# Storing the neighbour mask and the removed mask, and combining them and their transposes on TensorE

## The chip, the cores and the metric

The kernel runs on one core of a Trainium2 chip. The time is the device time of one execution in microseconds (us); lower is better. The engines named below are TensorE (PE; PEld is its weight load), VectorE (DVE), ScalarE (ACT), GpSimd (POOL) and SyncE (SP), whose queue issues all of the kernel's DMAs.

## What is computed

Four graph layers follow each other over 16 batch entries ("elements") of 1024 nodes with 64 features. The change concerns layer 0. It thins the adjacency matrix and then takes, for each node and feature, a weighted mean of three quantiles over the neighbours that are left:

```python
eye = jnp.eye(N, dtype=bool)
adj_ = jnp.where(eye[None], 1.0, adj)
nb = (adj_ > 0) & (~eye)[None]
m = nb.sum(-1)
rank = jnp.cumsum(nb, axis=-1) - 1
skip = jnp.where(m > T_THRESH, (m + K_DIL - 1) // K_DIL, 1)
do_dil = (skip > 1) & mask
removed = nb & do_dil[..., None] & ((rank + 1) % skip[..., None] == 0)
rem = removed | jnp.swapaxes(removed, 1, 2)
adj_d = jnp.where(rem, 0.0, adj_)
...
agg = _weighted_nanquantile_agg(x, adj_d > 0)
```

So an edge is dropped if either of its ends drops it, and the diagonal always stays. Each row drops at most two neighbours. Layers 1 to 3 (a degree-normalised sum, an attention with 8 heads, a linear graph layer) use the adjacency matrix as it came.

## The kernel before

Layer 0 of one element is 96 **compare steps**: 8 groups of features, times two halves of 512 nodes (`t`), times 6 quantile positions. A step makes three wide VectorE products (`le` L798, `wa` L800, `wb` L802), 17 matmuls into `prep` and `val`, two copies on ScalarE, and then `bit`, `pz` and `vs` with some delay. Between them stands the making of the tables (`px`, L710 to L741).

Everything else is interleaved with these steps by Python generators. In each step the loop in `picks` advances:

- the next tables (`coming`), twice;
- the **background** of the next element (`behind`), once. It consists of two generators: `ranking`, which sorts the features of a pair of elements (`ranks`; some 56 turns fall to each element), and `thinning`, which is `dilate`. While both have work, `going[n % 3 // 2]` gives two turns of three to `ranking` and one to `thinning`; when one ends, the other has every turn;
- in the last 12 steps of an element, the **stages** of the next one (`stages`), by the table `STEPS`. They call `neighbours` and `positions`;
- layers 1 to 3 of the element before (`layers`), by a due amount of 0.42 a step.

In the 12 steps before the end of an element the rest of the background is run out, if any is left. For the first element the background and its stages run ahead of the first step. A scheduler then orders the instructions of each engine from what was emitted; each engine and SP's queue take their instructions in that order.

**`dilate(b)`** works on 8 blocks of 128 rows. VectorE makes the mask `nb` of the neighbours without the diagonal (L453, L454), its running count `cum` (a scan, L456), and small columns: `m`, `do`, `mi` and `sk` (L459 to L470). From the row's count the columns `sk[:, 1:2]` and `sk[:, 2:3]` are made such that the entries to drop are those where |cum + sk1| equals sk2. ScalarE takes the absolute value (L471, recorded under the helper's line L379), VectorE compares (L474) and multiplies with `nb` (L475), which gives the mask `rem` of what this row drops. It is stored to `rem_d`. VectorE then subtracts `rem` from `nb` (L477) and adds the diagonal block (L478), and what is left is stored to `left_d`. The generator hands over after the absolute value, after L478 and after the last store: three times per block.

**`neighbours(left_d, rem_d, t)`** makes the mask that layer 0 uses, transposed: for each of 8 column blocks `j` a tile `valid[:, j, :]` of 128 x 512. It loads four 128 x 128 blocks of `left_d` (one DMA of 256-byte rows, L490) and a 128 x 512 piece of `rem_d` (L494) into one buffer `lr`. On TensorE, `minus_i` (the negative identity) takes `rem` into the PSUM tile `pn` as it lies (L499), and four matmuls with the blocks of `left` as weights and the identity as moving operand add the transposed rest (L504). ScalarE writes `valid` as the positive part of `pn`. There are 16 such groups per element, 256 in all.

`b2_` hands out buffers of a ring of six, which `nb`, `cum`, `rem`, `lr`, the sort's tiles and tiles of the layers share; `pb` hands out one of two PSUM tiles.

Of the kernel before, what the change touches and what calls it, by code (L numbers as in the profile page):

```python
# [8 lines left out]
F32 = mybir.dt.float32  # L9
BF = mybir.dt.bfloat16  # L10
# [6 lines left out]
OP = mybir.AluOpType  # L17
# [4 lines left out]
P = 128  # L22
# [16 lines left out]
def tile_preln_adj_stack(  # L39
# [30 lines left out]
    nc = tc.nc  # L70
    B, N, D = x.shape
    C = N // P
# [6 lines left out]
    const = ctx.enter_context(tc.tile_pool(name="const", bufs=1))  # L79
    dram = ctx.enter_context(tc.tile_pool(name="dram", bufs=2, space=DRAM))  # L80
# [13 lines left out]
    def b2_(name, shape=(P, 512), dt=F32):  # L94
        return sb.tile(list(shape), dt, tag="b2", bufs=6, name=name)
# [16 lines left out]
    def pb(name, shape=(P, 512), dt=F32):  # L112
        if alone and name != "pcols":
            return pa(name, shape, dt)
        return ps.tile(list(shape), dt, tag="pb", bufs=2, name=name)

    def small(name, shape, dt=F32, bufs=3):
        return sb.tile(list(shape), dt, tag="s_" + name, bufs=bufs, name=name)
# [26 lines left out]
    def scaled(name, shape, dt, src, scale):  # L145
        t = const.tile(list(shape), dt, name=name)
        nc.scalar.activation(t, src, AF.Copy, scale=scale)
        return t

    ident = scaled("ident", (P, P), HP, identf, 1.0)  # L150
    minus_i = scaled("minus_i", (P, P), BF, identf, -1.0)
    less = const.tile([P, 2, P], HP, name="less")
    nc.scalar.activation(less[:, 0, :], identf, AF.Copy, scale=-2.0)
    nc.scalar.activation(less[:, 1, :], identf, AF.Copy, scale=-FINE)

    NB = 7
    ci = sc("ci", (P, NB + 7), I32)
# [220 lines left out]
    def act(out_, in_, func=AF.Copy, **kw):  # L378
        nc.scalar.activation(out_, in_, func, **kw)  # L379

    def adjoining(made):

        first = next(made)
        with tc.issue_after(first.ins), tc.high_priority():
            for _ in made:
                pass
# [51 lines left out]
    def adj_rows(b, c):  # L438
        ad = sb.tile([P, N], F32, tag="adj", bufs=3, name="ad")
        nc.sync.dma_start(ad, adj[b, c * P : (c + 1) * P, :])  # L440
        return ad

    def dilate(b):

        left_d = dram.tile([C, P, N], BF, name="left_d")
        rem_d = dram.tile([C, P, N], BF, name="rem_d")
        for c in range(C):  # L450
            blk = slice(c * P, (c + 1) * P)
            nb = b2_("nb", (P, N), BF)
            nc.vector.tensor_scalar(nb, adj_rows(b, c), 0.0, None, op0=OP.is_gt)  # L453
            nc.vector.tensor_tensor(nb[:, blk], nb[:, blk], not_i, OP.mult)  # L454
            cum = b2_("cumn", (P, N), HP)
            nc.vector.tensor_tensor_scan(cum, nb, nb, 0.0, OP.add, OP.max)  # L456
            m = cum[:, N - 1 : N]
            do = small("do", [P, 1])
            nc.vector.tensor_scalar(  # L459
                do, m, float(T_THRESH), mask[:, b * C + c : b * C + c + 1], op0=OP.is_gt, op1=OP.mult  # L460
            )
            mi = small("mi", [P, 1], I32)
            nc.vector.tensor_scalar(mi, m, 1.0, None, op0=OP.add)
            nc.vector.tensor_scalar(mi, mi, 1, None, op0=OP.logical_shift_right)


            sk = small("sk", [P, 3])
            nc.vector.tensor_scalar(sk[:, 0:1], mi, 1.0, do, op0=OP.add, op1=OP.mult)
            nc.vector.tensor_scalar(sk[:, 1:2], sk[:, 0:1], -1.5, 1.5, op0=OP.mult, op1=OP.add)
            nc.vector.tensor_scalar(sk[:, 2:3], sk[:, 0:1], 0.5, -0.5, op0=OP.mult, op1=OP.add)  # L470
            act(cum, cum, AF.Abs, bias=sk[:, 1:2])  # L471
            yield
            rem = b2_("rem", (P, N), BF)
            nc.vector.tensor_scalar(rem, cum, sk[:, 2:3], None, op0=OP.is_equal)  # L474
            nc.vector.tensor_tensor(rem, rem, nb, OP.mult)  # L475
            nc.sync.dma_start(rem_d[c], rem)
            nc.vector.tensor_tensor(nb, nb, rem, OP.subtract)  # L477
            nc.vector.tensor_tensor(nb[:, blk], nb[:, blk], ident, OP.add)  # L478
            yield
            nc.sync.dma_start(left_d[c], nb)  # L480
            yield
        yield left_d, rem_d

    def neighbours(left_d, rem_d, t):

        hs = slice(t * 512, (t + 1) * 512)
        valid = sb.tile([P, C, 512], F8, tag=f"valid{t}", bufs=1, name="valid")
        for j in range(C):
            lr = b2_("lr", (P, 2, 512), BF)
            nc.sync.dma_start(  # L490
                lr[:, 0, :].rearrange("i (c j) -> i c j", c=4),
                left_d[4 * t : 4 * t + 4, :, j * P : (j + 1) * P].rearrange("c i j -> i c j"),
            )
            nc.sync.dma_start(lr[:, 1, :], rem_d[j, :, hs])  # L494

            pn = pb("pn")

            def made():
                yield nc.tensor.matmul(  # L499
                    pn, minus_i, lr[:, 1, :], start=True, stop=False, skip_group_check=True  # L500
                )
                for c in range(4):
                    cols = slice(c * P, (c + 1) * P)
                    yield nc.tensor.matmul(  # L504
                        pn[:, cols], lr[:, 0, cols], ident, start=False, stop=c == 3,
                        skip_group_check=True,
                    )

            adjoining(made())
            act(valid[:, j, :], pn, AF.Relu, saturate=False)  # L510
            if j < C - 1:
                yield None
        yield valid
# [437 lines left out]
    def background(b):  # L951
# [8 lines left out]
        def half():  # L960
            if b % 2 == 1 and b + 1 == B:
                return
            for r in rankings[(b + 1) // 2]:
                if r is None:
                    yield
                elif b:
                    return

        ranking, thinning, n = half(), dilate(b), 0
        going = [ranking, thinning]  # L970
        while going:
# [25 lines left out]
    def stages(el):  # L997
# [10 lines left out]
        for t in range(NH):  # L1008
            for r in neighbours(*masks, t):
                if r is None:  # L1010
                    yield
            el.valid.append(r)
            el.kq = next(where)
            yield
# [320 lines left out]
```

## Time and profile before

| | |
|---|---|
| median of 3 runs | 12517.13 us (12505.96 to 12527.63) |
| the profiled execution's own time | 12506.51 us |
| its span, first to last instruction | 12504.6 us |
| instructions in it | 216870 |
| mean granted TensorE clock | 0.970 |
| bytes moved by DMA | 908.06 MB, 73 GB/s on average |
| starts of the compare steps, first and last | 307.8 us and 12086.8 us |

The span has three parts. Up to 307.8 us the first element is sorted, thinned and turned. Then come 16 elements of 96 compare steps each. From 12086.8 us the layers of the last element run alone. An element in the middle takes about 733 us if its number is odd and about 762 us if it is even, since an even one has the first half of a sort in its background and an odd one the second half.

In the rows below, an engine's busy time counts overlapping instructions once. A row of a group gives line, engine, operation, output and input with their shapes, the count, then after the bar the summed busy time in us and the mean duration of one in ns, and then the idle time of the engine just before. A row of the timeline gives the start in us, the duration, the engine, the line and the operation, and in brackets how long the engine was idle before it and what ended that. A row of the windows gives from and to, the length, and per engine the busy time and in brackets the number of instructions, then the granted clock, the share of DMA time and GB/s. "SPq" is SP issuing a DMA.

### The profile page before, as it was taken

What the parts mean: (1) busy time and instruction counts of PE and PEld (TensorE: products, weight loads), DVE (VectorE), ACT (ScalarE), POOL (GpSimd) and SP (SyncE); (2) the same over time, 40 slices, a digit from 0 to 9 for tenths busy, and PEclk for the clock granted to TensorE, in tenths of its full rate; (3) what the DMA queues carried; (4) which work ended last, traced back from release to release, by engine and by line L of the source; (5) the groups of instructions that cost most, each with busy time, mean ns of one, the idle gap of its engine ahead of it and who ended that gap; (6) DMA issues with size and microseconds to landing.
All of it is one profiled execution on the core that took longest, in us unless ns stands there. A gap on an engine that the chain in (4) does not pass through costs nothing. (4 is left out here: it accounts for less than half of the span.)

```text
span 12504.6 us, 216870 instructions
## 1 busy us (share of the span) xinstructions
PE 11332.3 (91%) x85683; PEld 5376.8 (43%) x85697; DVE 11411.9 (91%) x17538; ACT 9572.4 (77%) x17160; POOL 3.2 (0%) x20
## 2 busy tenths in 40 slices
PE   3889999999999998999999999999999999999988
PEld 2334444444444444444444444444444444444445
DVE  8999989899998999989899998999989899988863
ACT  4877877778777887778777787777877778787866
POOL 0000000000000000000000000000000000000000
PEclk6999999999999999999999999999999999999989
DMA  7641121211212121121211212122121211201011
GB/s 237 239 135 54 54 76 57 72 62 59 72 56 77 57 66 64 53 80 57 79 52 60 75 55 75 55 69 66 56 73 54 82 55 59 80 31 56 32 51 59
DMA packets 520558, 908.06 MB, mean 73 GB/s; under 512 B 239728, under 2 KB 274672, under 8 KB 519536
## 3 DMA queue, kind: packets, MB, share of 16 engines
q1 hardware_dynamic: 519536, 894.18, 22.2%
q8 instruction: 672, 11.01, 0.4%
q14 instruction: 350, 2.87, 0.1%
HBM read 683.25 MB, written 206.57 MB: 71 GB/s over the span
## 5 line engine op out<-in xcount | busy, mean ns | idle before, releaser
L800 DVE TENSOR_TENSOR wa<-le,c 128x2048 f16<-128x2048 f16 x1536 | 1873.6, 1220 | 216.6 <-PE prep L821 150.1
L714 PE MATMUL px<-valid,cw 128*128 128x512 fp8e4 x8192 | 1961.8, 381 | 0.0
L802 DVE TENSOR_TENSOR wb<-le,c 128x2048 f16<-128x2048 f16 x1536 | 1872.1, 1219 | 0.0
L798 DVE TENSOR_TENSOR le<-cum,krow 128x2048 f16<-128x2048 int16 x1536 | 1868.8, 1217 | 0.4 <-ACT cum L379 0.4
L379 ACT ACTIVATE c<-px,shifts 128x512 f16<-128x512 f32 x2048 | 1424.9, 698 | 225.8 <-PE px L735 107.1
L1224 DVE CUSTOM_DVE_ANT_0 s<-sp,ad 128x1024 f32<-128x1024 f32 (+1 forms) x1024 | 1231.5, 1203 | 293.8 <-PE sp L1211 289.9
L379 ACT ACTIVATE s<-s,nm 128x1024 f32<-128x1024 f32 x1024 | 1185.4, 1158 | 273.9 <-DVE nm L1224 265.6
L714 PEld LDWEIGHTS <-cw 128*128 128x128 f16 x8192 | 800.4, 98 | 1083.3 <-issue 173.0
L1211 PE MATMUL sp<-kT,qT 64*128 64x512 f32 x4096 | 1230.9, 643 | 38.5 <-DVE nm L1224 35.9
L432 PE MATMUL pcols<-identf,s 128*128 128x128 f32 x8192 | 1160.2, 280 | 102.6 <-ACT s L379 64.1
L828 ACT COPY wi<-prep 128x512 f32<-128x512 f32 x1536 | 912.5, 594 | 413.6 <-PE prep L821 348.5
L435 ACT COPY eT<-pcols 128x512 f32<-128x512 f32 x2048 | 1128.6, 600 | 88.5 <-PE pcols L432 84.6
L432 PEld LDWEIGHTS pcols<-identf,s 128*128 128x128 f32 x8192 | 916.5, 141 | 578.6 <-ACT s L379 201.3
L821 PE MATMUL val<-le,tab 128*32 128x512 f16 x12288 | 1110.1, 389 | 23.8 <-ACT wi L828 13.7
L848 DVE SCALAR_TENSOR_TENSOR vs<-pz,vs 128x512 f32<-128x512 f32 x1536 | 1052.1, 685 | 83.4 <-PE pz L841 78.0
L379 ACT ACTIVATE high<-px,shifts 128x512 f16<-128x512 f32 x1024 | 709.2, 693 | 521.2 <-PE px L714 514.9
L1238 PE MATMUL ao<-eT,v 128*64 128x128 f32 x16384 | 1048.9, 277 | 31.7 <-ACT eT L435 26.3
L379 ACT ACTIVATE vs<-val 128x512 f32<-128x512 f32 x1536 | 939.7, 612 | 110.2 <-PE val L821 72.4
L1238 PEld LDWEIGHTS ao<-eT,v 128*64 128x64 f32 x16384 | 900.6, 137 | 280.9 <-ACT eT L435 149.9
L836 DVE TENSOR_SCALAR bit<-wi,to 128x512 int32<-128x512 int32 x1536 | 832.6, 542 | 4.7 <-ACT cw L379 3.6
L821 PE MATMUL prep<-wb,sel_w 128*32 128x512 f16 x6144 | 656.5, 396 | 189.9 <-DVE wb L802 183.7
L841 PE MATMUL pz<-bit,nth 128*128 128x512 bf16 x1522 | 611.1, 402 | 176.7 <-DVE bit L836 116.4
(262 smaller groups left out, 17794.5 us busy)
## 6 DMA issues: line engine op xcount, KB each, us to landing
ad<-in_adj_dram SPq DMA_DIRECT2D x768, 512.0 KB
aT<-adjT SPq DMA_DIRECT2D x256, 512.0 KB
adjT<-aT SPq DMA_DIRECT2D x128, 512.0 KB
md<-sm SPq DMA_DIRECT2D x216, 256.0 KB
sb<-md SPq DMA_DIRECT2D x216, 256.0 KB
rem_d<-rem SPq DMA_DIRECT2D x128, 256.0 KB
left_d<-nb SPq DMA_DIRECT2D x128, 256.0 KB
lr<-left_d SPq DMA_DIRECT2D x256, 128.0 KB
```

Source lines behind the costliest of these rows:

```text
L379: nc.scalar.activation(out_, in_, func, **kw)
L432: nc.tensor.transpose(pt[:, c, :], ad[:, (4 * s + c) * P : (4 * s + c + 1) * P], identf)
L435: nc.scalar.copy(aT[:, 4 * s : 4 * s + 4, :], pt)
L714: yield nc.tensor.matmul(px[pp], w[:, j, :], valid[:, j, :], start=False, stop=j == C - 1, skip_group_check=True,)
L798: nc.vector.tensor_tensor(le, cum, bc(el.krow[q][:, None, hs], [P, 4, 512]), OP.is_lt)
L800: nc.vector.tensor_tensor(wa, le, c0, OP.mult)
L802: last = nc.vector.tensor_tensor(wb, le, c1, OP.mult)
L821: yield nc.tensor.matmul(dst[32 * pp : 32 * pp + 32, :], w[pp], r[pp], start=i == 2, stop=i in (1, 3), tile_position=(0, 32 * pp), skip_gr ...
L848: nc.vector.scalar_tensor_tensor(vs, pz, 80.0, vs, op0=OP.is_equal, op1=OP.mult)
L1211: nc.tensor.matmul(sps[t], qT[t * D : (t + 1) * D, t ^ e, cols], kT[t * D : (t + 1) * D, e, :], start=True, stop=True,)
L1224: nc.vector.tensor_tensor_reduce(ss[e][:, hs], s, ad[:, hs], -1.0, nms[e] if hs.start else 3.0e38, op0=OP.add, op1=OP.min, accum_out=nm,)
L1238: nc.tensor.matmul(ao[e * D : (e + 1) * D, :], v[:, j, e * D : (e + 1) * D], eTs[e][:, j, :], start=j == 0, stop=j == C - 1, tile_position ...
```

## The change

In `dilate`, `nb` itself is stored, to `nb_d`, as soon as the absolute value has been asked for. The subtraction and the diagonal are gone from VectorE, and so is the third hand-over. The two instructions for `sk[:, 1:2]` and `sk[:, 2:3]` become one, with their constants in a tile `skip` that GpSimd fills once.

In `neighbours`, three DMAs per group replace two: the piece of `rem_d` as it lies goes to a buffer `cut` of its own, and `lr` holds four blocks of `nb_d` and the same four blocks of `rem_d`. TensorE adds to `pn`: minus `cut`; the identity, where the group holds the diagonal block (half of the groups); the transposed neighbours; and minus the transposed removed mask.

```diff
+    skip = const.tile([P, 4], F32, name="skip")
+    for i, w in enumerate((-1.5, 0.5, 1.5, -0.5)):
+        nc.gpsimd.memset(skip[:, i : i + 1], w)
...
-        left_d = dram.tile([C, P, N], BF, name="left_d")
+        nb_d = dram.tile([C, P, N], BF, name="nb_d")
         rem_d = dram.tile([C, P, N], BF, name="rem_d")
...
-            nc.vector.tensor_scalar(sk[:, 1:2], sk[:, 0:1], -1.5, 1.5, op0=OP.mult, op1=OP.add)
-            nc.vector.tensor_scalar(sk[:, 2:3], sk[:, 0:1], 0.5, -0.5, op0=OP.mult, op1=OP.add)
+            nc.vector.scalar_tensor_tensor(
+                sk[:, 1:3], skip[:, 0:2], sk[:, 0:1], skip[:, 2:4], op0=OP.mult, op1=OP.add
+            )
             act(cum, cum, AF.Abs, bias=sk[:, 1:2])
+            nc.sync.dma_start(nb_d[c], nb)
             yield
             rem = b2_("rem", (P, N), BF)
             nc.vector.tensor_scalar(rem, cum, sk[:, 2:3], None, op0=OP.is_equal)
             nc.vector.tensor_tensor(rem, rem, nb, OP.mult)
             nc.sync.dma_start(rem_d[c], rem)
-            nc.vector.tensor_tensor(nb, nb, rem, OP.subtract)
-            nc.vector.tensor_tensor(nb[:, blk], nb[:, blk], ident, OP.add)
             yield
-            nc.sync.dma_start(left_d[c], nb)
-            yield
-        yield left_d, rem_d
+        yield nb_d, rem_d
...
-    def neighbours(left_d, rem_d, t):
+    def neighbours(nb_d, rem_d, t):
...
+            cut = b2_("cut", (P, 512), BF)
+            nc.sync.dma_start(cut, rem_d[j, :, hs])
             lr = b2_("lr", (P, 2, 512), BF)
-            nc.sync.dma_start(
-                lr[:, 0, :].rearrange("i (c j) -> i c j", c=4),
-                left_d[4 * t : 4 * t + 4, :, j * P : (j + 1) * P].rearrange("c i j -> i c j"),
-            )
-            nc.sync.dma_start(lr[:, 1, :], rem_d[j, :, hs])
+            for s, part in enumerate((nb_d, rem_d)):
+                nc.sync.dma_start(
+                    lr[:, s, :].rearrange("i (c j) -> i c j", c=4),
+                    part[4 * t : 4 * t + 4, :, j * P : (j + 1) * P].rearrange("c i j -> i c j"),
+                )
...
                 yield nc.tensor.matmul(
-                    pn, minus_i, lr[:, 1, :], start=True, stop=False, skip_group_check=True
+                    pn, minus_i, cut, start=True, stop=False, skip_group_check=True
                 )
-                for c in range(4):
-                    cols = slice(c * P, (c + 1) * P)
+                if j // 4 == t:
                     yield nc.tensor.matmul(
-                        pn[:, cols], lr[:, 0, cols], ident, start=False, stop=c == 3,
+                        pn[:, j % 4 * P : (j % 4 + 1) * P], ident, ident, start=False, stop=False,
                         skip_group_check=True,
                     )
+                for s, turn in enumerate((ident, minus_i)):
+                    for c in range(4):
+                        cols = slice(c * P, (c + 1) * P)
+                        yield nc.tensor.matmul(
+                            pn[:, cols], lr[:, s, cols], turn, start=False,
+                            stop=s == 1 and c == 3, skip_group_check=True,
+                        )
```

## The prediction

> **What bounds the kernel now.** I read the page's engine totals first, then cut one element (one of the 16 batch entries) into stages, then looked at single rows and at the order of starts inside a stage. The totals decide nothing:
>
> ```profile
> PE 11332.3 (91%) x85683; PEld 5376.8 (43%) x85697; DVE 11411.9 (91%) x17538; ACT 9572.4 (77%) x17160; POOL 3.2 (0%) x20
> ```
>
> VectorE and TensorE are tied at 91%, and the change takes work from the one and gives work to the other. So the place matters. Every compare step issues one `le` (L798), and the timeline gives its starts; 96 of them make an element. For element 5 they give the windows below: steps 0-13, 14-47, 48-71, 72-80, 81-95.
>
> ```profile
> core 0: us, PE busy (x) PEld busy (x) DVE busy (x) ACT busy (x) POOL busy (x), PEclk, DMA share, GB/s
> 3953.00:4072.00 119.00, 104.02 (x774) 48.12 (x772) 107.50 (x181) 79.84 (x149) 0.00 (x0) 0.94 0.25 79
> 4072.00:4324.00 252.00, 238.65 (x1845) 111.91 (x1849) 251.09 (x402) 205.01 (x361) 0.00 (x0) 0.99 0.18 58
> 4324.00:4502.00 178.00, 168.53 (x1284) 78.11 (x1284) 176.88 (x290) 145.47 (x258) 0.00 (x0) 0.98 0.17 57
> 4502.00:4565.00 63.00, 58.27 (x458) 26.55 (x457) 62.83 (x99) 49.75 (x88) 0.00 (x0) 1.00 0.14 43
> 4565.00:4686.00 121.00, 116.37 (x938) 58.18 (x936) 98.18 (x143) 99.53 (x185) 0.00 (x0) 1.00 0.29 82
> ```
>
> From step 14 to step 80 VectorE is busy in 490.8 of 493 us: it is the bound. In the last 15 steps it is busy in 98 of 121, and TensorE in 116: there TensorE is the bound. The thinning of the next element (`dilate`) lies in the first kind of stretch, its transposes (`neighbours`, all 16 `pn` groups) in the second. Each edit therefore hits the engine that binds where it lands.
>
> **What it removes.** Per block of 128 rows, VectorE loses the subtraction and the diagonal, and two one-column instructions become one of two columns. The row means of the 128 calls are the upper price:
>
> ```profile
> L477 DVE TENSOR_TENSOR nb<-nb,rem 128x1024 bf16<-128x1024 bf16 x128 | 87.8, 686 | 0.0
> L478 DVE TENSOR_TENSOR nb<-nb,ident 128x128 bf16<-128x128 bf16 x128 | 28.2, 220 | 0.0
> ```
>
> But VectorE starts the next instruction before the record of the last one ends:
>
> ```profile
> 1017.08 0.69 DVE L477 TENSOR_TENSOR nb<-nb,rem 128x1024 bf16<-128x1024 bf16 x1
> 1017.68 1.22 DVE L802 TENSOR_TENSOR wb<-le,c 128x2048 f16<-128x2048 f16 x1
> 1018.82 0.22 DVE L478 TENSOR_TENSOR nb<-nb,ident 128x128 bf16<-128x128 bf16 x1
> 1018.95 0.69 DVE L848 SCALAR_TENSOR_TENSOR vs<-pz,vs 128x512 f32<-128x512 f32 x1
> ```
>
> Start to start they take 0.60 and 0.13 us, the small one 0.06 (L469 to L470 in the same view): 0.79 us per block, 6.4 per element, 102 in all; not the 134 of the means.
>
> **What it adds.** Each `pn` group gets four more 128-column matmuls, and half of the groups a fifth (identity on identity): 4.5 x 256 = 1152. In the last stage the groups follow each other like this:
>
> ```profile
> 3905.08 0.39 PE L499 MATMUL pn<-lr,minus_i 128*128 128x512 bf16 x1
> 3905.31 0.39 PE L504 MATMUL pn<-ident,lr 128*128 128x128 f16 x4
> 3905.53 0.38 PE L499 MATMUL pn<-lr,minus_i 128*128 128x512 bf16 x1
> ```
>
> A whole group takes 0.45 us, 0.23 before the four and 0.22 for them: 0.055 each. **A rule speaks for more**: the Trainium skill ("TensorE: Matmul & The Clock Gate", section "Back-to-back issue gap") gives about 81 ns per 128-column matmul in a stream in which every matmul has its own weight load, as here. By the rule the addition is 1152 x 0.081 = 93 us, by the row 1152 x 0.055 = 63 us, 4.0 per element. The row decides: it is this very instruction, with its weight loads beside it. Summed plainly, 102 off one engine against 63 on the other.
>
> **What it moves: the yields.** This is the larger part. `dilate` handed over three times per block (24 per element) and now twice (16). The background takes one turn per compare step and gives every third to thinning while both run. So thinning took 72 steps and now takes 48; the sort, which has some 56 turns per element, ended in step 79 and now ends in step 71. The compiled order of the changed program says the same: the scans of an odd element stood in steps 5, 12, 21, 30, 39, 48, 57, 65 and now stand in 5, 9, 15, 21, 27, 33, 39, 45. A block costs VectorE 5.2 us before and 4.4 after (its rows, start to start), a sort turn 3 x 0.60 = 1.8 forward or 4 x 0.33 = 1.3 backward. Per element:
>
> - Steps 0-47: 8 blocks of 4.4 instead of 5.3 of 5.2: +7.3 us on VectorE. Nearly all lies where it never rests; I count +6.4, the rest in the slack of steps 0-13.
> - Steps 48-71: 2.7 blocks fewer (-13.9), 8 sort turns more (+10.4 to +14.4): -3.5 or +0.5, mean -1.3.
> - Steps 72-80: 8 sort turns fewer, -10.4 to -14.4 on VectorE. But TensorE has 58.27 us of work in these 63; at the 96% that it reaches in the stage behind, it needs 60.7. So of some 12 us only 2.3 are gained.
> - Steps 81-95: +4.0 on TensorE, the bound, in full.
>
> **Buffers and queues.** `cut` and `lr` now take two buffers of the ring of six that `lr` alone had, so loads run three masks ahead, not six, with three issues each on SP's queue instead of two (0.42 us each). The shortest way from issue to use shows at the start:
>
> ```profile
> 166.97 0.39 SPq L490 DMA_DIRECT2D lr<-left_d  x1
> 167.41 0.56 SPq L494 DMA_DIRECT2D lr<-rem_d  x1
> 169.84 0.61 PE L499 MATMUL pn<-lr,minus_i 128*128 128x512 bf16 x1 [24.77 <-DMA lr<-rem_d]
> ```
>
> 2.4 us after the last issue. A freed buffer becomes a full one after 3 x 0.42 + 2.4 = 3.7 us. In the compiled order, groups 8, 9 and 10 stand together and group 11 comes about 1.9 us of TensorE work after group 8: a wait of 1.8 us, with the prep and val matmuls of the step queued behind it, and through them ACT's copies and VectorE's next `bit`. The other groups have a step or more between them. Bounds: 0 if the scheduler's spacing suffices, 5 us if several groups wait; I take 1.5. Before, TensorE waited 0.6 us for `lr` in all elements after the first. SP's `adj` loads stand behind these issues; I count nothing for them, since DMA engines are busy in 0.29 of that window, up to 2 us per element if they come late. The earlier store of `nb` is one DMA either way and is waited for only some 40 steps later. Four constants on GpSimd: nothing.
>
> **The sum.** Elements 1 to 13: 6.4 - 1.3 - 2.3 + 4.0 + 1.5 = +8.3 each, 108. Element 0: TensorE is busy in only 543 of its 650 us, so the freed steps are gained: -3. Element 14 thins alone (24 turns become 16), the saving of 6 and the crowding about cancel; its `pn` groups cost +4. Start: VectorE is busy in 128.6 of the 129 us from 31 to 160, and its eight blocks save 6. In all +103. The profiled execution has a span of 12504.6 and took 12506.5: **12610 us**. The median of the runs, 12517.1, lies 11 higher, and on it the sum would be 12620; I stay with the execution that I counted.
>
> **Rivals.**
> - *Faster: VectorE's saving is banked where it is made.* If steps 72-95 behave as one stretch in which TensorE catches up, crowding earlier costs nothing: the element gains 6.4 and pays 4.0. 16 x -6.4 + 63 = -39: 12467. For it: sums over whole elements show nothing else. Against it: TensorE already works 92% of steps 72-80, so it has little to catch up. It decides if steps 72-80 shrink by over 10 us.
> - *No change.* Half of that catching up: steps 72-80 give 7 instead of 2.3, and no buffer waits: about +2 per element, 12530 at most.
> - *Much slower: the ring of three.* Waits for `cut` and `lr` of 5 us or more per element instead of 1.5, late `adj` loads among them: +50 to +80 on the sum, 12660 to 12690.
> - That the change doesn't do what it says: the stored difference is gone, and the signs add up to neighbours minus both removed masks plus the diagonal; I give it nothing.
>
> **Chances.** Forecast 0.50, much slower 0.20, no change 0.14, faster 0.16. A measurement of this kernel tells 0.2% (25 us) from nothing. The range reaches from the middle of the faster and no-change cases, 12480, to 12690.
>
> **What would show it.** Steps 14-47 of an element about 6 us longer with VectorE still over 99% busy; in steps 72-80 VectorE well under 90% busy while the stage shrinks by no more than 5 us; `pn` groups of about 0.7 us, and new TensorE waits on `cut` or `lr` of 1 to 2 us per element. I am wrong if steps 72-80 shrink by 10 us, or if the last stage does not grow by the 4 us of matmuls.

## The result, and the profile after

| | before | after |
|---|---|---|
| median of the runs | 12514.97 us (12505.96 to 12527.63, 6 runs) | 12596.73 us (12583.54 to 12607.68, 6 runs) |
| profiled execution | 12506.51 us | 12607.68 us |
| ratio of the times | | 1.0063 [1.0051, 1.0075] |

The changed kernel is slower by 82 us. The two profiled executions lie 101 us apart, since that of before is one of the shortest of its runs and that of after the longest; the parts below are measured between these two. The page of after gives the span and the engine totals:

```profile
span 12605.9 us, 219690 instructions
PE 11454.3 (91%) x86849; PEld 5450.3 (43%) x86849; DVE 11337.1 (90%) x17154; ACT 9592.3 (76%) x17160; POOL 3.4 (0%) x24
```

VectorE's busy time fell by 75 us and TensorE's rose by 122, so the saving and the addition are both there. Again the totals don't tell what they are worth. The windows of after for element 5, cut at the same five groups of compare steps as before (steps 0-13, 14-47, 48-71, 72-80, 81-95; columns: stretch, length, then busy time and count of each engine, granted clock, DMA share, GB/s):

```profile
3987.00:4107.50 120.50, 105.13 (x768) 47.45 (x766) 109.17 (x181) 78.59 (x147) 0.00 (x0) 0.93 0.25 82
4107.50:4369.70 262.20, 248.03 (x1874) 114.87 (x1872) 257.91 (x414) 210.06 (x369) 0.00 (x0) 1.00 0.20 65
4369.70:4541.70 172.00, 162.61 (x1259) 76.00 (x1256) 170.95 (x277) 140.28 (x251) 0.00 (x0) 1.00 0.14 46
4541.70:4599.90 58.20, 56.64 (x447) 26.27 (x445) 51.73 (x68) 48.57 (x85) 0.00 (x0) 1.00 0.20 54
4599.90:4731.30 131.40, 128.06 (x1027) 64.13 (x1027) 101.96 (x149) 103.66 (x192) 0.00 (x0) 1.00 0.32 88
```

Steps 14-47 take 262 us instead of 252, with VectorE still busy in 98% of them: the crowding. Steps 72-80 shrink from 63 to 58 and VectorE is now busy in only 89% of them. The last stage grows from 121 to 131 and is TensorE's for 97%. Taking the same cuts in all elements gives, as after minus before in us:

| steps | 0-13 | 14-47 | 48-71 | 72-80 | 81-95 | element |
|---|---|---|---|---|---|---|
| foreseen for elements 1 to 13 | 0 | +6.4 | -1.3 | -2.3 | +5.5 | +8.3 |
| mean of elements 1 to 13 | -0.7 | +7.5 | -1.8 | -10.2 | +11.2 | +6.1 |
| odd elements | +2.3 | +9.1 | -5.1 | -5.6 | +10.4 | +11.1 |
| even elements | -4.2 | +5.7 | +2.1 | -15.6 | +12.3 | +0.3 |

Thirteen elements make +79. The start adds 4, element 0 adds 11, element 14 adds 4 and what follows it 2: together the 101.

The largest change of a stage, -15.6 and +12.3 in the even elements, is in part one amount of work on two sides of a border. These are the windows of element 6 for steps 72-80 and 81-95, first before, then after:

```profile
5262.10:5329.50 67.40, 62.80 (x467) 28.08 (x459) 67.40 (x95) 55.03 (x98) 0.00 (x0) 1.00 0.23 72
5329.50:5448.60 119.10, 113.37 (x891) 55.84 (x888) 95.95 (x140) 91.08 (x170) 0.00 (x0) 1.00 0.29 85
```

```profile
5312.10:5363.90 51.80, 48.38 (x388) 22.74 (x387) 50.07 (x67) 40.88 (x73) 0.00 (x0) 1.00 0.21 60
5363.90:5495.20 131.30, 127.95 (x1026) 64.02 (x1026) 99.81 (x143) 102.74 (x189) 0.00 (x0) 1.00 0.33 93
```

TensorE's busy time fell by 14.4 us in the first window and rose by 14.6 in the second. Not all of this is the same work. The second window again with the `pn` matmuls alone (and ScalarE's reading of `pn`), before and then after:

```profile
5329.50:5448.60 119.10, 9.02 (x80) 9.10 (x16) 1.00 0.29 85
```

```profile
5363.90:5495.20 131.30, 14.95 (x152) 9.34 (x16) 1.00 0.33 93
```

Of the 135 matmuls that the second window has more, 72 are the change's own, busy for 5.9 us. The other 63, some 9 us, have come over from earlier steps: the first window lost 79. The windows are cut where VectorE starts a compare step. VectorE hurries through steps 72-80 because the sort is gone from them, and a part of TensorE's work of that time is done in the last stage, where TensorE is the bound.

The `pn` groups in the timeline of after (start, duration, engine, line, operation):

```profile
4667.61 0.38 PE L503 MATMUL pn<-cut,minus_i 128*128 128x512 bf16 x1
4667.83 0.39 PE L514 MATMUL pn<-ident,lr 128*128 128x128 f16 x4
4668.05 0.39 PE L514 MATMUL pn<-minus_i,lr 128*128 128x128 bf16 x4
4668.27 0.38 PE L503 MATMUL pn<-cut,minus_i 128*128 128x512 bf16 x1
```

From start to start a group takes 0.66 us, 0.22 for each set of four, as foreseen. The new waits are another matter. The longest waits of TensorE for these loads (us in total, times, longest), first at the start of before (up to 308 us), then at the start of after (up to 312 us), then in after from there to the end:

```profile
PE pn L499 <- DMA lr<-rem_d: 49.5, 9, 24.8
```

```profile
PE pn L503 <- DMA cut<-rem_d: 33.9, 6, 19.0
```

```profile
PE pn L514 <- DMA lr<-nb_d: 1.4, 3, 0.6
```

After the first element's preparation TensorE's matmuls wait 1.4 us for these loads in all, not 1.5 us per element. Its weight loads, which run ahead, do meet late buffers (some 19 us in all for `lr` and `cut`, 1.2 before), but 17 of the 19 lie beside matmuls that are still running. There the matmuls are not bound by the ring of three.

### The profile page after: what moved, and what is told of

It reads as the page before. It is cut to its first block, busy times and chain, and to the rows that moved or that the text cites. A ratio compares the mean times of both kernels' runs of the same rounds, so it can differ in the third digit from the quotient of the medians.

```text
span 12605.9 us, 219690 instructions
## 1 busy us (share of the span) xinstructions
PE 11454.3 (91%) x86849; PEld 5450.3 (43%) x86849; DVE 11337.1 (90%) x17154; ACT 9592.3 (76%) x17160; POOL 3.4 (0%) x24
## 4 chain that ended last, share of the span: by engine, by line
DVE 40%; PE 39%; ACT 9%; issue 5%; DMA 2%; ACTq 0%; SPq 0%; DVEq 0%
DVE wa L810 6%; PE px L724 6%; DVE wb L812 6%; DVE le L808 6%; DVE s L1234 4%; PE ao L1248 4%; PE sp L1221 3%; PE prep L831 3%; DVE vs L858 3%; PE pcols L436 3%; PE val L831 3%; DVE bit L846 2%; PE two L1072 2%; PE agg L864 2%; ACT s L383 2%
## 5 line engine op out<-in xcount | busy, mean ns | idle before, releaser
L383 ACT ACTIVATE low<-px,shifts 128x512 f16<-128x512 f32 x1024 | 713.4, 700 | 73.3 <-PE px L736 71.7
```

## Experiments

The prediction's sum has three large parts: what VectorE saves, what TensorE and the loads add, and the hand-over that is lost (with the early store of `nb` at nothing). Each was undone or done alone. Ratios are against the kernel before. Stage numbers are from the profiled executions, as in the table above.

### The hand-over given back (three_turns)

The changed kernel with a third hand-over, so that thinning takes 72 steps again:

```diff
             nc.sync.dma_start(rem_d[c], rem)
+            yield
             yield
```

> The changed kernel with a third hand-over per block put back, bare, so that thinning again takes 72 steps and the sort ends near step 79. Theory (the lost hand-over crowds VectorE's work into steps where it is the bound): the crowding goes, VectorE keeps its saving of 6.4 us per element, of which about 6 lie in steps 14-71, and TensorE's 4 to 5 us per element stay in the last stage: about 2 us per element less than before, 12480 to 12495, ratio to before 0.997 to 0.999; steps 14-47 of an odd element near 248 us instead of 262, steps 72-80 back at 63. Rival (the extra matmuls and loads are the whole loss, hand-overs don't matter): 12570 to 12600, ratio 1.005.

Measured: 12545.32 us, 1.0025 [1.0015, 1.0034], between the two ranges that were expected. The hand-over is worth some 50 us in the changed kernel, the larger part of its loss. But with it given back the kernel is still slower by 32, where the theory had it faster: the crowding makes the loss larger and is not all of it. By stage (0-13 to 81-95) the elements show -0.9, -2.9, +0.6, -0.7 and +6.7: the crowding is gone, and the last stage keeps more than the 4 us of matmuls.

### The hand-over taken away alone (two_turns_alone)

The kernel before, with all of its work:

```diff
             nc.vector.tensor_tensor(nb[:, blk], nb[:, blk], ident, OP.add)
-            yield
             nc.sync.dma_start(left_d[c], nb)
             yield
```

> The kernel before with its middle and last hand-over merged, so that each block hands over twice; nothing else of the change. Theory: steps 0-47 get 8 blocks of 5.2 us instead of 5.3 of them, +13 us on VectorE; steps 48-71 -1, steps 72-80 about -10, the last stage +6 of TensorE work that is pushed there: +8 per element, 12600 to 12640, ratio 1.007 to 1.010, slower than the changed kernel. Rival (hand-overs don't matter): within 0.2% of before.

Measured: 12609.64 us, 1.0074 [1.0062, 1.0087], +97, as the theory has it. No instruction was added. The stages show +5.2, +13.1, -3.5, -9.3 and +2.1 us: more than the expected 13 in steps 0-47, and in the last stage less than the expected 6. Steps 14-47 of element 6 in the windows, before and then here:

```profile
4818.30:5079.50 261.20, 244.60 (x1849) 112.70 (x1846) 259.70 (x376) 206.12 (x367) 0.00 (x0) 1.00 0.16 55
```

```profile
4859.50:5133.60 274.10, 251.01 (x1859) 114.98 (x1858) 270.71 (x408) 216.31 (x377) 0.00 (x0) 0.99 0.18 59
```

VectorE has 11 us more to do in the same 34 steps and is busy in 99% of both.

### More hand-overs (four_turns, four_turns_vector_path)

If crowding costs, spreading should gain. The first is the changed kernel with four hand-overs per block, one added behind the scan and one behind the store of `rem`. The second is the kernel before with a fourth behind the scan, for all elements but the first; its edit is shown:

```diff
+            if b:
+                yield
```

> The changed kernel with four hand-overs per block (a bare one after the scan, a bare one at the end), so that thinning lasts 84 steps and sort and thinning end together. Theory: VectorE's background falls from 1.6 to 1.4 us a step in steps 0-71 and is level up to step 83; steps 14-71 lose about 10 us per element until TensorE (95% busy there) is the bound, the last stage gains 4 to 5: 12400 to 12460, ratio 0.991 to 0.996. Rival (TensorE is the true bound of steps 14-71 already): not below the kernel with three hand-overs.

> The kernel before with a fourth hand-over per block (bare, after the scan) for all elements but the first: nothing of the change. Theory (level VectorE background where VectorE binds): steps 14-71 of even elements lose about 8 us as they did with four hand-overs in the changed kernel, the last stage gets the sort's last turns, where VectorE has 20 us to spare: 12430 to 12490, ratio 0.993 to 0.998. Rival (the gain was given back in the last stage, as it was for odd elements there): within 0.2% of before.

Measured: four_turns 12513.86 us, 1.0000 [0.9992, 1.0009]; four_turns_vector_path 12497.39 us, 0.9984 [0.9978, 0.9991]. The direction holds in both, and both gain less than was expected. The changed kernel goes from +82 by +32 to no difference as its hand-overs go from two to four. Against the theory that VectorE alone decides stands that in four_turns the last stage of odd elements still grows by 15 us and the start by 24. The other version is faster than both kernels and shares nothing with the change.

### The added TensorE work and the added loads (matmuls_alone, loads_and_ring_alone, matmuls_and_loads)

To the kernel before were added the four or five matmuls of a group, with a moving tile of zeros; then the third load with `cut` and `lr` in two buffers of the ring, without the matmuls; then both:

```diff
-                for c in range(4):
...
+                for s, turn in enumerate((ident, nought)):
+                    for c in range(4):
```

```diff
+            cut = b2_("cut", (P, 512), BF)
+            nc.sync.dma_start(cut, rem_d[j, :, hs])
             lr = b2_("lr", (P, 2, 512), BF)
...
+            for s, part in enumerate((left_d, rem_d)):
```

> The kernel before with the changed kernel's extra matmuls (4 or 5 per group, against a tile of zeros, so they add nothing) and with the loads, the buffers, VectorE's work and the three hand-overs of before. The kernel with three hand-overs and VectorE's work kept was 136 us over before, where the counted matmuls are 63. If the matmuls' own time is what the last stage pays: +4.0 to 4.7 per element and +3 at the start, 12575 to 12590, ratio 1.005 to 1.006. If they carry all of the 136 (switches between kinds of matmul, order): ratio 1.010 to 1.011. If they are hidden: 1.000 to 1.002.

> The kernel before with the changed kernel's three loads per group and its two tiles of the ring (the second half of lr is loaded but not read), and with the five matmuls of before. If the ring of three and SP's longer queue cost what the matmuls don't explain: the start 10 to 20 us later, and 2 to 4 us per element, ratio 1.003 to 1.006. If the loads only matter at the start, where DMA engines are busy 0.8 of the time: +10 to +20, ratio 1.001 to 1.002. By the prediction's 1.5 us per element: +20 to +25, ratio 1.002.

> The kernel before with both additions that were tried singly: the three loads in two tiles of the ring, and the extra matmuls (the second half of lr against zeros, so they add nothing). VectorE's work and the stores of dilate are those of before. Singly they cost 31 and at most 8 us. If they add: 12545 to 12565, ratio 1.002 to 1.004. If together they cost what the kernel with three hand-overs and VectorE's work kept did: 12640, ratio 1.010 to 1.011. In the first case that kernel's other 100 us come from how its unused VectorE work stands in dilate, and not from TensorE.

Measured: matmuls_alone 12547.06 us, 1.0025 [1.0017, 1.0033], +31; loads_and_ring_alone 12521.74 us, 1.0007 [0.9998, 1.0015]; matmuls_and_loads 12576.59 us, 1.0047 [1.0034, 1.0061], +61. TensorE's busy total rose by 66.8 us in the first of these, 58 ns for each of 1152 matmuls, yet the time rose by half of that: in the last stage +4.4 us in odd and only +0.8 in even elements. With the loads beside them it is +8.1 and +5.2, and steps 14-80 stay as they were, within 0.5 us in the means. So the two together cost about what the matmuls were counted at, but not only in the stage they were put in: the last stage pays 6.7 us in the mean, 3.1 come back in steps 0-13 behind it, and the start pays 17. Why the last stage takes in half of the matmuls when they come alone, and not when the loads are there too, is not settled.

The loads also cost at the start: 18.8 us with the loads alone and 16.6 with both.

### VectorE's work taken out alone (no_vector_work)

The kernel before, without L477 and L478 and with the one small instruction for two. Layer 0 of this kernel uses another mask, since nothing subtracts `rem` from `nb`.

```diff
-            nc.vector.tensor_tensor(nb, nb, rem, OP.subtract)
-            nc.vector.tensor_tensor(nb[:, blk], nb[:, blk], ident, OP.add)
```

> The kernel before without the subtraction and the diagonal on VectorE, and with the merged small instruction: the neighbour mask itself is stored, so layer 0 takes another mask; hand-overs, loads and matmuls of before. Theory (each of the 102 us is saved where VectorE binds): 12415 to 12440, ratio 0.992 to 0.994. If TensorE, 95% busy there, takes over at once: 12490 to 12510, ratio 0.998 to 0.9995; then the kernel with three hand-overs, 32 us over before, is explained by about 40 us of additions less about 10 of saving.

Measured: 12461.95 us, 0.9956 [0.9943, 0.9968], -54: half of the 102, and between the two ranges that were expected. Steps 14-47 of an element are shorter by 3.0 us in the mean (4.8 in odd elements, 0.9 in even ones), not 6.4. The window of steps 14-47 of element 6 (that of before is shown above), and the wait that grew most, over all elements, before and then here:

```profile
4791.50:5051.10 259.60, 241.78 (x1836) 113.41 (x1833) 255.01 (x364) 202.98 (x361) 0.00 (x0) 1.00 0.16 53
```

```profile
DVE s L1224 <- PE sp L1211: 161.8, 107, 3.6
```

```profile
DVE s L1227 <- PE sp L1214: 196.2, 130, 3.6
```

VectorE's work in this window fell by 4.7 us and the window by 1.6; VectorE's idle time in it went from 1.5 to 4.6. Over all elements it waits 34 us more for the attention's scores `sp` from TensorE. So an engine that is busy in 99% of a stretch doesn't turn each microsecond of removed work into a microsecond of time. TensorE has not simply become the bound in its place: it is busy for 241.78 of these 259.6 us, 93%, against 94% before, so some 18 us are free. What VectorE waits for are single results of TensorE. The compiled order of VectorE's other instructions in this window has changed as well, and how much of the missing saving is due to that is not known.

### The saving measured on the changed side, and the early store (three_turns_vector_work_kept, vector_work_kept_on_cum, early_store_alone)

The first of these is three_turns with the two VectorE operations and the two small instructions put back, their result unused. The second is the same, but the operations work on `cum`, which no DMA reads. The third is the kernel before with the store of `nb` at the place where the change has it; layer 0 there takes another mask, since what is stored is not yet the difference.

```diff
             act(cum, cum, AF.Abs, bias=sk[:, 1:2])
+            nc.sync.dma_start(left_d[c], nb)
             yield
...
-            nc.sync.dma_start(left_d[c], nb)
             yield
```

> The changed kernel with three hand-overs, and with VectorE's subtraction, diagonal and two small instructions kept though nothing uses their result: TensorE's and the queue's part of the change alone. Theory: +4 us of matmuls and up to 1.5 us of waits per element in the last stage, where TensorE is the bound: 12575 to 12600, ratio 1.005 to 1.007; VectorE's saving is then the distance to the kernel with three hand-overs, about 90 us. Rival 1 (TensorE's addition is hidden): ratio 1.000 to 1.002. Rival 2 (the ring of three and the late loads cost more than the matmuls): ratio over 1.009.

> As the kernel with three hand-overs and VectorE's work kept, but the unused subtraction and diagonal are done in place on cum instead of on nb, whose store is under way. If that kernel's 136 us came from work on a tile whose store it has to wait for: ratio 1.002 to 1.004. If they are the cost of the additions when VectorE has its full load: ratio 1.009 to 1.012.

> The kernel before with the store to left_d moved ahead of the first hand-over, so that it stores the neighbour mask itself, as the changed kernel does; subtraction and diagonal stay on VectorE, unused, and layer 0 takes another mask. The two kernels with VectorE's work kept were 133 and 142 us over before, and the kernel with the extra matmuls and loads alone 61; they differ in this store and its place. If the early store itself costs the difference: 12580 to 12610, ratio 1.005 to 1.007, with steps 14-71 about 5 us longer per element. If only all parts together make the worse order of instructions: within 0.2% of before.

Measured: 12648.86 us, 1.0110 [1.0095, 1.0126]; 12657.95 us, 1.0111 [1.0097, 1.0125]; and 12584.55 us, 1.0055 [1.0041, 1.0069]. The first was expected at 1.007 at most, so something besides matmuls and loads costs here. It is not that the subtraction has to wait until the store has read `nb`, since on `cum` the time is the same. The third run shows it: with the work of before and only the store moved, 72 us are lost, and three quarters of what an element loses lie in steps 48-71:

| steps | 0-13 | 14-47 | 48-71 | 72-80 | 81-95 |
|---|---|---|---|---|---|
| early_store_alone | +1.0 | +0.9 | +4.5 | -0.7 | +0.4 |
| matmuls_and_loads | -3.1 | +0.5 | 0.0 | 0.0 | +6.7 |
| three_turns_vector_work_kept | -2.0 | +0.3 | +4.8 | -0.8 | +7.1 |
| no_vector_work | +2.5 | -3.0 | +0.2 | -1.2 | -0.8 |
| three_turns | -0.9 | -2.9 | +0.6 | -0.7 | +6.7 |

Rows one and two add up to row three within 1.1 us in every stage, and within 0.3 in steps 48-71. Rows two and four add up to row five within 0.8, and within 0.4 in steps 48-71, with nothing left over there for row one: **where the subtraction is gone, as in the change, the early store leaves no trace** in steps 48-71. This is read from sums of stages, and no run has the early store without the subtraction and nothing else. Over the whole kernel three_turns costs 32 us where its two parts give 61 - 54 = 7. These 25 us are about as large as the uncertainty of that sum (some 26), so a cost of the early store in other places isn't ruled out. The windows of steps 48-71 of element 6, before and with the early store:

```profile
5079.50:5262.10 182.60, 168.16 (x1282) 77.89 (x1280) 181.65 (x270) 144.04 (x252) 0.00 (x0) 1.00 0.16 53
```

```profile
5109.00:5296.70 187.70, 174.78 (x1286) 79.83 (x1286) 184.18 (x270) 145.86 (x256) 0.00 (x0) 1.00 0.16 54
```

VectorE's counts are the same and TensorE's nearly so, but TensorE's busy time is 6.6 us longer and VectorE idles 3.5 us instead of 1.0. Within these steps VectorE's passes over the scores and over `bit` and `vs` stand in a different compiled order. That this order is the cause is only argued; why a DMA that is emitted earlier changes it stays open. The changed kernel with a late store of `nb` wasn't tried. Since each edit can change the compiled order, the cost of any part measured alone may hold an effect of this kind, and no run here separates it.

### The kernel before, once more (before_again)

> The kernel before itself, as a control for the stage times and the durations of VectorE's instructions on this chip: ratio 0.999 to 1.001, wa near 1218 to 1225 ns in the mean.

Measured: 12511.73 us, 0.9998 [0.9990, 1.0006]. Its profile repeats every stage of the elements within 0.4 us in the means, while the start came out 2.9 us longer, element 0 shorter by 7.1 and element 14 by 3.8. So half a microsecond in the stage tables can be read, and a few us at the start or in element 0 can't. The start of the change (+4) and its element 0 (+11) are therefore weak numbers.

## Why the prediction was right, and where its terms were off

**The total and the place.** 12610 was foreseen, 12596.73 came, and the sum of +103 stands against +101 between the profiled executions and +82 between the medians. That the lost hand-over costs by crowding is shown: alone it costs 97, and in the changed kernel some 50 of its 82. That it turns the sign is not so. In the prediction's sum the change without this loss gains 19 us (103 - 122); with the hand-over given back it measured 32 slower.

The three large terms, done alone, against what the prediction counted:

| part | counted | measured alone |
|---|---|---|
| VectorE's work removed | -102 | -54 [-71, -40] |
| matmuls, loads and ring | +83 (63, and 1.5 x 13 of waits) | +61 [+43, +76] |
| hand-over lost (the rest of the sum) | +122 | +97 [+78, +109] |
| sum | +103 | +104 |

The brackets are the ratios' intervals in us. Their widths, taken together, leave the sum of the singles uncertain by some 28, so that it agrees with the measured +82 [+64, +94]. That the total came so near is luck, since errors cancelled: **the saving was counted almost twice too large (by 48), and the two costs too large by 22 and 25**. Nor do the singles add up stage by stage: in elements 1 to 13 they give +4.6, +10.6, -3.3, -10.5 and +8.0, together +9.4, where the change has +6.1. So the parts act on each other. In the changed kernel the hand-over is worth some 50, not 97; what the saving is worth beside two hand-overs was not measured.

- *VectorE's saving.* The step that failed is "From step 14 to step 80 VectorE is busy in 490.8 of 493 us: it is the bound", taken to mean that all work removed there is time gained. The engine rested more as soon as it had less to do. Of the 102, the busy total of the run without this work shows 77 (11334.8 against 11411.9); against these stand 34 more of waiting for `sp`, and the profiled execution came out 45 shorter, the median 54.
- *The hand-over.* In steps 0-47 the prediction sets 8 blocks of 4.4 us where 5.3 would stand, +11.9; the changed kernel against three_turns has +10.6 there, so the crowding itself was sized well. What comes free behind it was undervalued: -1.8 counted in steps 48-95 (+0.5 and -2.3), against -2.4, -9.5 and +4.5, which is -7.4. Per element that leaves +3.2, not +10. Of its parts the most wrong is "of some 12 us only 2.3 are gained": it came to 5.0 in steps 72-95.
- *Steps 14-47.* +6.4 counted, +7.5 measured, right in size; VectorE is busy in 98% of them in element 5, where the prediction asked for over 99%.
- *Steps 48-71.* -1.3 counted (the mean of its two figures, -3.5 and +0.5, is -1.5), -1.8 measured.
- *Steps 72-80 and 81-95.* The prediction said that it would be wrong if steps 72-80 shrank by 10 us, and they did. The rival tied to this mark, that the saving is banked where it is made, is refuted in its total (12467), but for these stages it is about half right. Of the +11.2 in the last stage, 6.7 come with the matmuls and loads alone. Against three_turns the last stage grew by 4.5 while steps 72-80 shrank by 9.5; with the hand-over alone it grew by 2.1 while they shrank by 9.3. So the argument that VectorE gets ahead and TensorE pays for it holds for a half or less of the freed time. The mark was badly set too: it looked at one side of a border that TensorE's work crosses. Taken together the two stages give +1.0 where +3.2 was counted.
- *Matmuls.* 0.22 us per four as foreseen, so the row held and not the 81 ns of the Trainium skill ("TensorE: Matmul & The Clock Gate", "Back-to-back issue gap"): by the busy total of matmuls_alone 58 ns each. That is near the 56 ns which the same section gives for a single matmul, with nothing counted for its weight load. In the time, they cost 31 us alone and 61 with the loads.
- *Waits for the ring of three.* 1.5 us per element counted, 1.4 us in all measured behind the first element. This term was wrong. The loads are late by about as much as was thought (19 us of waiting weight loads are some 1.2 per element), but it was assumed that the matmuls stand still for it, and they had work left.
- *The start.* -6 counted, +4 measured. The windows from 160 to 240 us, before and after:

```profile
160.00:240.00 80.00, 36.30 (x182) 22.49 (x182) 68.12 (x153) 29.98 (x54) 0.00 (x0) 0.67 0.80 252
```

```profile
160.00:240.00 80.00, 51.40 (x226) 30.15 (x225) 56.46 (x130) 42.06 (x75) 0.00 (x0) 0.59 0.89 276
```

VectorE, which sorts here, is busy for 56 us instead of 68. That the third load and its buffers cost at the start is shown by the two runs that have them (+19 and +17 there, where the repeated kernel before moved by 2.9). The sum had no term for it. Full DMA engines are not shown to be the reason: they are busy in 0.89 of this window instead of 0.80, but in matmuls_and_loads in only 0.77 of it. Nor are TensorE's waits, which are shorter than before (33.9 us for `cut`, against 49.5 for `lr`). What is new is a wait of VectorE, here in matmuls_and_loads:

```profile
DVE sr L598 <- PE pn L504: 7.2, 5, 3.9
```

`sr` is a tile of the sort. It takes its buffer from the same ring of six, and here it waits until TensorE has read one for `pn`. With the loads alone this wait is 9.3 us, in after 2.2, and before it doesn't show. So the ring does bind at the start, through VectorE; what makes the rest of the 17 to 19 us is open.

- *The early store, at nothing.* True in steps 48-71 of the changed kernel as far as the sums of stages tell, and 72 us wrong in a kernel that keeps the subtraction.

## What to carry to other kernels

Where background work is metered by turns, count the turns before the operations: dropping one hand-over of three, with no instruction added, cost 97 us alone, where all of the added matmuls and loads cost 61. Don't count work that is taken off an engine which is 99% busy as time gained in full: here half of it came, though the next engine, 94% busy, had room left. Measure the saving alone before you set it against a cost. To test a claim about a stage, add up the stages on both sides of its border, since another engine's work may have crossed it, and tell that work from what the change itself adds there.

## What the runs showed of the hardware that was not expected

A 128-column matmul costs by its neighbours. Where the compiled order mixes the `pn` groups with the attention's matmuls, the timeline of after shows single ones:

```profile
4686.90 0.23 PE L514 MATMUL pn<-minus_i,lr 128*128 128x128 bf16 x1
4687.06 0.43 PE L1248 MATMUL ao<-eT,v 128*64 128x128 f32 x2
4687.42 0.23 PE L514 MATMUL pn<-minus_i,lr 128*128 128x128 bf16 x1
```

Here one takes 0.16 us from its start to the start of the next matmul, where four in a row take 0.22 together. Over the whole trace of after, the mean is 0.158 us for the 70 that stand before an `ao` matmul (f32, weights of 64 columns) and 0.155 for the 64 before `val` (f16, weights of 32 columns), but 0.062 for the 46 before `pz` (weights of 128 columns, as its own). Why is not shown.

And the same instructions can load TensorE differently: with the early store alone its busy total in the profile is 76 us higher (11408.2 against 11332.3) at nearly the same number of matmuls (85695 and 85683 recorded).
